# Layer 1's weighted sums on column tiles of 64 and 32 instead of 65 columns in one piece

## The chip, the cores and the metric

The kernel runs on one core of a Trainium2 chip. The metric is device time in microseconds (us), smaller is better. A core has five engines that run their own instruction streams side by side: TensorE (PE, matrix products into the accumulation memory PSUM; its weight loads are listed apart as PEld), VectorE (DVE), ScalarE (ACT), GpSimd (POOL) and SyncE (SP, which only issues transfers here). Semaphores tie the streams together.

## The reference

A stack of four graph layers over 4096 nodes with 64 features and one 4096 x 4096 adjacency of zeros and ones. Every layer normalises x, applies a ReLU, computes something from the neighbours and adds it to x. The change concerns layer 1, which works on every pair of nodes in hyperbolic space:

```
x_t     = logmap0(x, c)
left    = x_t @ w_att[:D, 0];  right = x_t @ w_att[D:, 0]
adj_att = sigmoid(left[:, None] + right[None, :] + b_att[0]) * adj
x_local = logmap(x[:, None, :], x[None, :, :], c)
support_t = einsum('ij,ijd->id', adj_att, x_local)
return proj(expmap(x, support_t, c), c)
```

The 64-vector `logmap(x_i, x_j)` is a scalar that depends on the pair times a combination of x_i and x_j. So the einsum becomes, for every node i, a sum over j of (weight of the pair) times a row of 65 numbers of node j: its 64 features and one more from its squared norm. The distance part of the weight is the same for (i, j) and (j, i); the sigmoid and the adjacency are not. Layers 0, 2 and 3 are not touched.

## The kernel before

Layer 0 takes the first 1240 us, layer 1's pairs 1240 to 1832 us, a chain of VectorE work on the nodes (`finish`) up to about 1904 us, layers 2 and 3 the rest. All times here are counted in the profiled execution.

The pairs are computed in `pairs_fast`. The nodes form 8 groups of 512 (`G`), each four blocks of 128 (`GB` = 4). A job is a pair of groups (gi, gj) with gj <= gi, 36 jobs in all: 28 off the diagonal and 8 on it. Each job computes the symmetric factor once, in four steps that the code writes as functions over batches of two jobs:

- `scores` / `weights_of`: mask and attention logits go to PSUM by two matmuls per block (`pl`, lines 2194 and 2197), and ScalarE takes the sigmoid into `sg`, for both directions of the pair.
- `distances`: four f32 matmuls (`pu`, line 2225), clipped by VectorE (line 2232) and combined (line 2233).
- `factors`: four wide passes on ScalarE and two on VectorE (lines 2247 and 2252) give the factor `F_`.
- `sums`: VectorE multiplies the weights by the factor (line 2260). Four f32 matmuls with the 65-column rows of the source nodes as weights (`XQ`, the same tile as `VQ`) add into `acci` (line 2262). Off the diagonal the factor is transposed block by block on TensorE (`pf`, line 2277), multiplied into the weights of the other direction (line 2280), and four more matmuls add into `accj` (line 2281); VectorE then adds `accj` to `VT` (line 2288). When the diagonal job closes group gi, `acci` is copied to `VT` (line 2270).

`VT` holds the 65 sums in partitions 0 to 64 and the nodes along the free dimension. After the pairs it is brought back to nodes-in-partitions form by 32 transposes (line 2312), and VectorE scales the result into `VQ` (line 2314).

The PSUM pools hold two buffers each for `pu`, `pl` and `pf`, and one each for `acci` and `accj`.

The order of the instructions on TensorE and VectorE is not the order of these lines. The framework's scheduler places each engine's instructions by its own costs; only ScalarE's activations (`act`) are held in program order. TensorE's stream around the sums is therefore an interleaving of `pl`, `pu`, `pf`, `acci` and `accj` work.

An f32 matmul is two instructions in the profile ("pieces" below), each with its own weight load, which is why the 144 matmuls of line 2262 appear as 288.

Of the kernel before, what the change touches and what calls it, by code (L numbers as in the profile page):

```python
# [9 lines left out]
F32 = mybir.dt.float32  # L10
# [8 lines left out]
ALU = mybir.AluOpType  # L19
# [5 lines left out]
P = 128  # L25
N = 4096
NB = N // P
D = 64
G = 512
NG = N // G  # L30
GB = G // P
# [799 lines left out]
def kernel(  # L831
# [24 lines left out]
    nc = tc.nc  # L856
# [7 lines left out]
    D1 = D + 1  # L864
# [10 lines left out]
    ident = cpool.tile([P, P], F32, name="ident")  # L875
# [45 lines left out]
    def over(col, width):  # L921

        return col.unsqueeze(2).to_broadcast([P, col.shape[1], width])
# [75 lines left out]
    with ExitStack() as l0:  # L999
# [281 lines left out]
        with ExitStack() as pa:  # L1281
            hp = pa.enter_context(tc.tile_pool(name="prep", bufs=1))
            work = pa.enter_context(tc.tile_pool(name="pwork", bufs=2))
# [47 lines left out]
            with in_order():  # L1331
                nc.vector.tensor_reduce(fsum, FT[0:F, :], AX.X, ALU.add)
                for b0 in range(0, NB, 8):
                    pw = (ps, ps2)[b0 // 8 % 2].tile([P, 8, KZ], F32, name="pst", tag="misc")
                    for b in range(8):
                        nc.tensor.matmul(
                            pw[:, b, :],
                            lhsT=FT[:, (b0 + b) * P : (b0 + b + 1) * P],
                            rhs=rhz,
                            start=True,  # L1340
                            stop=True,
# [19 lines left out]
                for g in range(HW // G):  # L1361
                    pr = (ps, ps2)[g % 2].tile([P, G], F32, name="psr", tag="misc")
                    nc.tensor.matmul(
                        pr, lhsT=srep, rhs=FT[:, g * G : (g + 1) * G], start=True, stop=True
# [27 lines left out]
                for k in range(2):  # L1392
                    pr = ps.tile([P, G], F32, name="prs", tag="misc")
                    for q in range(4):
# [3 lines left out]
                            lhsT=rs,  # L1398
                            rhs=FT[:, g * G : (g + 1) * G],
                            start=True,  # L1400
                            stop=True,
# [23 lines left out]
        with ExitStack() as ha:  # L1425
            hp = ha.enter_context(tc.tile_pool(name="heads", bufs=2))
            work = ha.enter_context(tc.tile_pool(name="hwork", bufs=1))
# [32 lines left out]
            for hf in range(2):  # L1460
# [9 lines left out]
                for hd in range(NH):  # L1470
                    first = hd == 0
# [47 lines left out]
                    def add_up(acc, values, moving, start, stop):  # L1519
                        for k in range(NS):  # L1520
                            ins = nc.tensor.matmul(  # L1521
                                acc[k * O : (k + 1) * O, :],
                                lhsT=values,
                                rhs=moving(k),
                                start=start,
                                stop=stop,
                            )
                        return ins.ins
# [3 lines left out]
                    for j0 in range(0, NB, 2):  # L1532
# [19 lines left out]
                        for i, j in enumerate(range(j0, j0 + 2)):  # L1552
                            for n, (acc, y) in enumerate(parts):
# [4 lines left out]
                                    start=j == 0 and (n == 0 or acc is not parts[n - 1][0]),  # L1558
                                    stop=j == NB - 1 and (acc is not accB or n == len(parts) - 2 - spatial),
                                )  # L1560
                        for i, j in enumerate(range(j0, j0 + 2)):
                            for c in range(2):
# [5 lines left out]
                                    start=j == 0 and c == 0,  # L1568
                                    stop=False,
                                )  # L1570
                                if whole:
# [4 lines left out]
                                        start=False,  # L1576
                                        stop=False,
                                    )
                            if first:
                                with behind(sums):  # L1580
# [6 lines left out]
                                        start=(j == 0),  # L1587
                                        stop=(j == NB - 1),
# [15 lines left out]
                    if first:  # L1604
# [3 lines left out]
                        pf = ps.tile([P, GB, NS, NH], F32, name="pf", tag="misc")  # L1608
                        for b in range(GB):
                            nc.tensor.matmul(  # L1610
                                pf[:, b].rearrange("p q h -> p (q h)"),
                                lhsT=dsum[:, b * P : (b + 1) * P],
                                rhs=fold_f.rearrange("p q h -> p (q h)"),
                                start=True,
                                stop=True,
# [11 lines left out]
                    for c in range(2):  # L1627
                        for k in range(NS):
                            nc.tensor.matmul(
                                accC[k * O : (k + 1) * O, :],  # L1630
                                lhsT=meanq[k * O : (k + 1) * O, hd, c, :],
                                rhs=em4[k * O : (k + 1) * O, :],
                                start=False,
                                stop=c == 1,
# [92 lines left out]
        with ExitStack() as ob:  # L1727
            hp = ob.enter_context(tc.tile_pool(name="outatt", bufs=1))
            work = ob.enter_context(tc.tile_pool(name="owork", bufs=2))
# [44 lines left out]
            with in_order():  # L1774
# [67 lines left out]
                for k in reversed(range(NK)):  # L1842
                    r = (NK + k) * O
# [68 lines left out]
            for u in range(4):  # L1912
# [8 lines left out]
                for q in range(NQ):  # L1921
# [10 lines left out]
                    for t in range(0, JT, 2):  # L1932
# [12 lines left out]
                        for acc, Y, E in products:  # L1945
                            for i in range(2):
                                for k in range(NK):
                                    sums = nc.tensor.matmul(
                                        acc[k],
                                        lhsT=Y[:, i].rearrange("p s d -> p (s d)"),  # L1950
                                        rhs=E[:, i, k * G : (k + 1) * G],
                                        start=j0 + i == 0,
                                        stop=acc is accB and j0 + i == NB - 1,
                                    )
                    with behind(sums.ins):
                        for t in range(JT):
                            j = q * JT + t
                            fl = dict(start=(j == 0), stop=(j == NB - 1))
                            for k in range(NK):
# [3 lines left out]
                                    lhsT=YD1[:, j],  # L1963
                                    rhs=B2[t // 2][:, t % 2, ks],
# [4 lines left out]
                                    lhsT=YD2[:, j],  # L1969
                                    rhs=m[:, t, ks].bitcast(F8),  # L1970
# [14 lines left out]
                for k in range(NK):  # L1985
                    nc.tensor.matmul(
                        accC[k],
                        lhsT=meano[NK * O :, k].rearrange("p s d -> p (s d)"),
                        rhs=em[NK * O :],
                        start=False,  # L1990
                        stop=True,
# [114 lines left out]
    def pairs_fast(es, VQ):  # L2106

        fp = es.enter_context(tc.tile_pool(name="pf", bufs=1))
        XQ = VQ
# [11 lines left out]
        with ExitStack() as ss:  # L2121
# [16 lines left out]
            pt = ps.tile([3 * NB, P], F32, name="ppt", tag="misc")  # L2138
# [10 lines left out]
            for dst, k in ((XA, 0), (LD, 1)):  # L2149
# [11 lines left out]
                for g in range(NG):  # L2161
# [4 lines left out]
                        ps,  # L2166
                        nc.scalar.copy,
                    )
        VT = fp.tile([D1, N], F32, name="VT")
        work = es.enter_context(tc.tile_pool(name="pfwork", bufs=2))  # L2170
        with ExitStack() as ss:
            ps_u = ss.enter_context(tc.tile_pool(name="ps_u", bufs=2, space=PSUM))
            ps_l = ss.enter_context(tc.tile_pool(name="ps_l", bufs=2, space=PSUM))
            ps_f = ss.enter_context(tc.tile_pool(name="ps_f", bufs=2, space=PSUM))
            ps_a = ss.enter_context(tc.tile_pool(name="ps_a", bufs=1, space=PSUM))

            def grp(g):
                return slice(g * G, (g + 1) * G)
# [30 lines left out]
            accs, sig, tiles = {}, {}, {}  # L2209
# [26 lines left out]
            def factors(batch):  # L2236
# [12 lines left out]
                for job in batch:  # L2249
                    at, xt = tiles[job]  # L2250
                    act(at, at, AF.Ln, bias=one_t, scale=1.0)
                    nc.vector.scalar_tensor_tensor(at, at, TMAX, xt, ALU.min, ALU.mult)

            def sums(batch):
                for gi, gj in batch:
                    F_ = tiles.pop((gi, gj))[0]
                    if gj == 0:
                        accs[gi] = ps_a.tile([D1, G], F32, name="acci", tag="acci")
                    w = sig.pop((gi, gj))
                    nc.vector.tensor_tensor(w, w, F_, ALU.mult)  # L2260
                    for b in range(GB):
                        nc.tensor.matmul(  # L2262
                            accs[gi],
                            lhsT=XQ[:, gj * GB + b, :],
                            rhs=w[:, b, :],
                            start=(gj == 0 and b == 0),
                            stop=(gi == gj and b == GB - 1),
                        )
                    if gi == gj:
                        nc.vector.tensor_copy(VT[:, grp(gi)], accs.pop(gi))  # L2270
                        continue
                    w = sig.pop((gj, gi))
                    accj = ps_a.tile([D1, G], F32, name="accj", tag="accj")
                    for t in range(GB):
                        pf = ps_f.tile([P, G], F32, name="pf", tag="pf")
                        for b in range(GB):
                            nc.tensor.transpose(
                                pf[:, b * P : (b + 1) * P], F_[:, b, t * P : (t + 1) * P], ident
                            )
                        nc.vector.tensor_tensor(w[:, t, :], w[:, t, :], pf, ALU.mult)  # L2280
                        nc.tensor.matmul(
                            accj,
                            lhsT=XQ[:, gi * GB + t, :],
                            rhs=w[:, t, :],
                            start=(t == 0),
                            stop=(t == GB - 1),
                        )
                    nc.vector.tensor_tensor(VT[:, grp(gj)], VT[:, grp(gj)], accj, ALU.add)


# [13 lines left out]
                    distances(batches[n + 2])  # L2304

        nc.vector.tensor_scalar(pabs, pabs, sqc, 2.0, ALU.mult, ALU.mult)
        with tc.tile_pool(name="ps_vt", bufs=2, space=PSUM) as ps:
            for g in range(NG):
                pt = ps.tile([P, GB, D1], F32, name="pvt", tag="misc")
                for b in range(GB):  # L2310
                    c = (g * GB + b) * P
                    nc.tensor.transpose(pt[:, b, :], VT[:, c : c + P], ident[:D1, :D1])
                bs = slice(g * GB, (g + 1) * GB)
                nc.vector.tensor_tensor(VQ[:, bs, :], pt, over(pabs[:, bs], D1), ALU.mult)

# [333 lines left out]
    with tc.If(general == 0):  # L2649
        after_pairs(pairs_fast)  # L2650
        with ExitStack() as es:
            layers_fast(es)
        nc.vector.tensor_reduce(bad[:, 0:1], bad, AX.X, ALU.add)
        odd = spool.tile([P, 1], F32, name="odd")
        nc.gpsimd.partition_all_reduce(odd, bad[:, 0:1], P, RMAX)
        nc.vector.tensor_scalar(again, odd, 0.0, None, ALU.is_gt)
# [57 lines left out]
```

## Time and profile before

| | us |
|---|---|
| median of 3 runs (2250.61 to 2261.21) | 2261.08 |
| the profiled execution's own time | 2264.45 |
| its span | 2262.7 |
| stretch of the pairs, 1240 to 1832 us | 592 |
| of this: TensorE busy | 549.1 |
| VectorE busy | 504.9 |
| ScalarE busy | 488.4 |

The span is the time from the first to the last instruction on the profiled core. "Busy" of TensorE is the union of its matmul records; their ends are modelled, so what is trustworthy is the distance from the start of one record to the start of the next. A row of a group gives line, engine, operation, output and inputs, shapes as partitions x elements, the count, busy time and mean duration, then the idle time of the engine just before these instructions and what ended it. "128*65" in a row of TensorE is contraction by columns used of the array.

### The profile page before, as it was taken

The page shows a single profiled execution, that of the slowest core. Times are in us where ns is not written, and L with a number is a line of the kernel's source. Part 1 is how long each engine was busy: PE and PEld are TensorE (multiplying, and loading weights), DVE is VectorE, ACT ScalarE, POOL GpSimd, SP SyncE. Part 2 cuts the span into 40 slices and gives each one's busy share as a digit, 9 for nine tenths or more (in the row PEclk, how much of TensorE's full clock was granted, in tenths as well). Part 3 has the DMA queues.
Part 4 walks back from the last instruction along what each step waited for, and adds up shares of the span by engine and source line. Part 5 has one row for each costly group of instructions (what it writes and reads, how often), then busy time and mean ns, then how long its engine had stood idle before and what let it go on. Part 6 is the DMA issues. An engine that isn't in the chain of part 4 may idle for free. (4 is left out here: it accounts for less than half of the span.)

```text
span 2262.7 us, 42590 instructions
## 1 busy us (share of the span) xinstructions
PE 1938.4 (86%) x18732; PEld 904.9 (40%) x18732; DVE 1770.1 (78%) x2074; ACT 1589.8 (70%) x1338; POOL 86.0 (4%) x124
## 2 busy tenths in 40 slices
PE   4989989999999999859992799999999933959998
PEld 3444444444444544423441244434344411434332
DVE  6689989987898899797657888888898889544552
ACT  4678878996898899467752888879788920114775
POOL 1000100100000000001101000000000000000000
PEclk8999999999999999879995899999999966965999
DMA  9945554352111020477530001100110005724993
GB/s 112 181 89 104 90 90 114 123 190 93 44 63 63 26 75 2 132 247 264 188 122 20 20 23 33 38 24 28 33 33 26 26 0 204 301 82 140 332 332 119
DMA packets 117002, 238.92 MB, mean 106 GB/s; under 512 B 11059, under 2 KB 84003, under 8 KB 102051
## 3 DMA queue, kind: packets, MB, share of 16 engines
q1 hardware_dynamic: 101990, 192.92, 24.6%
q0 software_dynamic: 14816, 43.18, 10.8%
q8 instruction: 148, 2.42, 0.4%
q14 instruction: 48, 0.39, 0.1%
HBM read 245.34 MB, written 49.46 MB: 130 GB/s over the span
## 5 line engine op out<-in xcount | busy, mean ns | idle before, releaser
L1185 ACT ACTIVATE st<-srow,nt 128x2048 int8<-128x2048 f32 x352 | 682.8, 1994 | 81.6 <-DVE B L1191 80.8
L1191 DVE TENSOR_TENSOR B<-st,mres 128x1024 int32<-128x1024 int32 x256 | 312.0, 1221 | 71.8 <-PE accC L1521 44.6
L1521 PE MATMUL accB<-B,ybh 128*32 128x512 fp8e4 x3072 | 340.5, 385 | 15.6 <-DVE B L1191 15.6
L1521 PE MATMUL accD<-B,ybh 128*32 128x512 fp8e4 x2048 | 302.6, 388 | 23.6 <-DVE h L1637 23.6
L1521 PEld LDWEIGHTS <-ybh 128*32 128x32 bf16 (+1 forms) x6656 | 197.5, 98 | 240.8 <-issue 79.8
L1521 PE MATMUL accC<-B,ycn 128*32 128x512 fp8e4 x2272 | 267.8, 380 | 1.2 <-issue 1.2
L1521 PE MATMUL accC<-mres,ych 128*32 128x512 fp8e4 x2272 | 268.0, 381 | 0.0
L1521 PE MATMUL accL<-B,ybh 128*32 128x512 fp8e4 x1536 | 221.4, 391 | 4.8 <-DVE h L1641 4.7
L1521 PEld LDWEIGHTS <-ych 128*32 128x32 f16 x4096 | 169.0, 99 | 116.5 <-issue 11.9
L929 DVE SCALAR_TENSOR_TENSOR raw<-raw 128x2048 f32<-128x2048 f32 x64 | 146.4, 2289 | 79.3 <-DMA raw<-in_adj_dram 79.1
L1179 DVE TENSOR_SCALAR st<-srow,nt 128x2048 uint8<-128x2048 f32 x160 | 205.6, 1285 | 2.5
L2181 ACT ACTIVATE sg<-pl,rb 128x512 f32<-128x512 f32 x256 | 163.6, 684 | 53.7 <-PE pl L2197 50.6
L1185 ACT ACTIVATE st<-srowo,nto 128x1024 int8<-128x1024 f32 x128 | 137.3, 1137 | 42.1 <-DVE B L1191 42.1
L2225 PE MATMUL pu<-XAf,LDf 66*128 66x512 f32 x288 | 151.4, 630 | 13.7 <-DVE at L2232 12.5
L2607 ACT ACTIVATE w3b<-pv 128x1024 int16<-128x1024 f32 x128 | 131.1, 1024 | 45.6 <-PE pv L2598 45.3
L1521 PE MATMUL accC<-C,ych 128*32 128x512 fp8e4 x1824 | 148.3, 393 | 1.4 <-DVE C L1199 1.4
L1199 DVE TENSOR_TENSOR C<-B,mres 128x1024 int32<-128x1024 int32 x114 | 139.6, 1225 | 3.6
L2262 PE MATMUL acci<-sg,VQ 128*65 128x512 f32 x288 | 137.8, 602 | 4.8 <-DVE sg L2260 4.6
L1521 PEld LDWEIGHTS <-ycn 128*32 128x32 f16 x2272 | 107.6, 97 | 64.0 <-issue 3.1
L2416 PE MATMUL nacc<-m,HH 128*128 128x512 fp8e4 x256 | 62.0, 391 | 74.6 <-ACT HH L2405 74.6
L2232 DVE TENSOR_SCALAR at<-pu 128x512 f32<-128x512 f32 x144 | 95.2, 685 | 26.2 <-PE pu L2225 26.2
L2194 PE MATMUL pl<-nm,noid 128*128 128x512 fp8e4 x256 | 101.0, 395 | 11.8 <-ACT sg L2181 11.7
(488 smaller groups left out, 3124.3 us busy)
## 6 DMA issues: line engine op xcount, KB each, us to landing
raw<-in_adj_dram SPq DMA_DIRECT2D x64, 1024.0 KB, 6.9
mo<-edges SPq DMA_DIRECT2D x32, 512.0 KB, 4.7
noedge<-nmo POOLq DMA_DIRECT2D x32, 512.0 KB, 4.3
nm<-noedge SPq DMA_DIRECT2D x64, 256.0 KB, 3.1
m<-edges SPq DMA_DIRECT2D x16, 1024.0 KB, 5.2
m<-edges SPq DMA_DIRECT2D x32, 512.0 KB, 5.0
srow<-srow_d SPq DMA_DIRECT2D x15, 1024.0 KB, 6.6
mres<-in_adj_dram POOLq DMA_DIRECT2D x8, 1024.0 KB, 35.7
```

Source lines behind the costliest of these rows:

```text
L929: nc.vector.scalar_tensor_tensor(raw, raw, 0.0, raw, ALU.is_gt, ALU.not_equal, accum_out=bad[:, c : c + 1])
L1179: nc.vector.tensor_scalar(st[:, i, :].bitcast(U8), srow, negs[:, i : i + 1], EDGE, ALU.is_gt, ALU.mult)
L1185: nc.scalar.activation(st[:, i, :], srow, AF.Sign, bias=negs[:, i : i + 1], scale=-1.0)
L1191: nc.vector.tensor_tensor(B.bitcast(I32), st.bitcast(I32), edges.bitcast(I32), ALU.bitwise_and)
L1199: nc.vector.tensor_tensor(C.bitcast(I32), B.bitcast(I32), edges.bitcast(I32), ALU.bitwise_xor)
L1521: ins = nc.tensor.matmul(acc[k * O : (k + 1) * O, :], lhsT=values, rhs=moving(k), start=start, stop=stop,)
L2181: tc.keep_in_program_order(nc.scalar.activation(*args, **kw))
L2194: nc.tensor.matmul(pl, lhsT=noid, rhs=nm[:, b, :].bitcast(F8), start=True, stop=False)
L2225: nc.tensor.matmul(pu, lhsT=LD[:, j * P : (j + 1) * P], rhs=XA[:, grp(gi)], start=True, stop=True,)
L2232: nc.vector.tensor_scalar(at[:, b, :], pu, UMIN, None, ALU.max)
L2262: nc.tensor.matmul(accs[gi], lhsT=XQ[:, gj * GB + b, :], rhs=w[:, b, :], start=(gj == 0 and b == 0), stop=(gi == gj and b == GB - 1),)
L2607: nc.scalar.activation(w, pv, AF.Relu)
```

## The change

`VT` becomes a tile of 128 partitions. A helper `add_up` issues one matmul either with the 64 feature columns of a source block (`row` is None: 64 output rows at partition `low`, a column tile of 64) or with columns 33 to 64 of its row (32 output rows at partition `row`, a column tile of 32), of which only the last, the 65th, is of use.

Off the diagonal, `accj` has the features of one direction in partitions 0 to 63 and the 32-wide tiles in partitions 64 and 96; `acci` has the features of the other in partitions 64 to 127 and the 32-wide tiles in partitions 0 and 32. For every block t the two 64-wide matmuls stand behind each other in the code, and after every second block the four 32-wide ones. On the diagonal both accumulators are used too: even blocks go to `accj`, odd ones to `acci`. When a diagonal job closes a group, two copies of 64 partitions bring `acci` to `VT` with its halves exchanged, and `accj` is added as in the other jobs.

The 32 transposes of `VT` become 32 f32 matmuls with a 128 x 65 matrix `fold_v` that adds the two halves and picks the two rows of the 65th column; two small VectorE instructions build it.

```diff
-        VT = fp.tile([D1, N], F32, name="VT")
+        VT = fp.tile([P, N], F32, name="VT")
...
+            def add_up(acc, low, row, src, w, start, stop):
+                cols, r, n = (slice(0, D), low, D) if row is None else (slice(D1 - 32, D1), row, 32)
+                nc.tensor.matmul(
+                    acc[r : r + n, :], lhsT=XQ[:, src, cols], rhs=w, start=start, stop=stop
+                )
...
-                    for b in range(GB):
-                        nc.tensor.matmul(
-                            accs[gi],
-                            lhsT=XQ[:, gj * GB + b, :],
-                            rhs=w[:, b, :],
...
                     if gi == gj:
-                        nc.vector.tensor_copy(VT[:, grp(gi)], accs.pop(gi))
-                        continue
+                        for b in range(0, GB, 2):
+                            j = gj * GB + b
+                            add_up(accj, 0, None, j, w[:, b], b == 0, b == GB - 2)
+                            add_up(acci, D, None, j + 1, w[:, b + 1], gi == 0 and b == 0, b == GB - 2)
                         for b in range(GB):
+                            j = gj * GB + b
+                            r = b // 2 * 32
+                            if b % 2:
+                                add_up(acci, 0, r, j, w[:, b], gi == 0, True)
+                            else:
+                                add_up(accj, 0, D + r, j, w[:, b], True, True)
+                        accs.pop(gi)
+                        nc.vector.tensor_copy(VT[0:D, grp(gi)], acci[D : 2 * D])
+                        nc.vector.tensor_copy(VT[D : 2 * D, grp(gi)], acci[0:D])
+                    else:
+                        v = sig.pop((gj, gi))
+                        for t in range(GB):
...
+                            nc.vector.tensor_tensor(v[:, t, :], v[:, t, :], pf, ALU.mult)
+                            first = gj == 0 and t == 0
+                            add_up(accj, 0, None, gi * GB + t, v[:, t], t == 0, t == GB - 1)
+                            add_up(acci, D, None, gj * GB + t, w[:, t], first, False)
+                            if t % 2:
+                                for k in range(2):
+                                    c = t - 1 + k
+                                    last = c + 2 >= GB
+                                    add_up(accj, 0, D + k * 32, gi * GB + c, v[:, c], t == 1, last)
+                                    add_up(
+                                        acci, 0, k * 32, gj * GB + c, w[:, c], gj == 0 and t == 1, False
+                                    )
                     nc.vector.tensor_tensor(VT[:, grp(gj)], VT[:, grp(gj)], accj, ALU.add)
...
+        fold_v = work.tile([P, D1], F32, name="fold_v", bufs=1)
+        nc.vector.tensor_copy(fold_v[:, 0:D], ident[:, 0:D])
+        nc.vector.tensor_tensor(
+            fold_v[:, D:], ident[:, D + 31 : D + 32], ident[:, P - 1 :], ALU.add
+        )
...
-                    nc.tensor.transpose(pt[:, b, :], VT[:, c : c + P], ident[:D1, :D1])
+                    nc.tensor.matmul(
+                        pt[:, b, :], lhsT=VT[:, c : c + P], rhs=fold_v, start=True, stop=True
+                    )
```

More of the change, by code (lines that the diff above doesn't have):

```diff
@@ L2257, in sums @@
                     if gj == 0:
-                        accs[gi] = ps_a.tile([D1, G], F32, name="acci", tag="acci")
+                        accs[gi] = ps_a.tile([P, G], F32, name="acci", tag="acci")
+                    acci = accs[gi]
+                    accj = ps_a.tile([P, G], F32, name="accj", tag="accj")
                     w = sig.pop((gi, gj))
                     nc.vector.tensor_tensor(w, w, F_, ALU.mult)
-                    for b in range(GB):
-                        nc.tensor.matmul(
-                            accs[gi],
-                            lhsT=XQ[:, gj * GB + b, :],
-                            rhs=w[:, b, :],
-                            start=(gj == 0 and b == 0),
-                            stop=(gi == gj and b == GB - 1),
-                        )
@@ L2269, in sums @@
-                    if gi == gj:
-                        nc.vector.tensor_copy(VT[:, grp(gi)], accs.pop(gi))
-                        continue
[L2272 to L2275, printed above, removed]
-                        for b in range(GB):
[L2277 to L2287, printed above, removed]
+                    if gi == gj:
+                        for b in range(0, GB, 2):
+                            j = gj * GB + b
+                            add_up(accj, 0, None, j, w[:, b], b == 0, b == GB - 2)
+                            add_up(acci, D, None, j + 1, w[:, b + 1], gi == 0 and b == 0, b == GB - 2)
+                        for b in range(GB):
+                            j = gj * GB + b
[10 more added lines that the diff above has]
+                        for t in range(GB):
+                            pf = ps_f.tile([P, G], F32, name="pf", tag="pf")
+                            for b in range(GB):
+                                nc.tensor.transpose(
+                                    pf[:, b * P : (b + 1) * P], F_[:, b, t * P : (t + 1) * P], ident
+                                )
[11 more added lines that the diff above has]
+                                    )
@@ L2311, in pairs_fast @@
                     c = (g * GB + b) * P
-                    nc.tensor.transpose(pt[:, b, :], VT[:, c : c + P], ident[:D1, :D1])
+                    nc.tensor.matmul(
+                        pt[:, b, :], lhsT=VT[:, c : c + P], rhs=fold_v, start=True, stop=True
+                    )
                 bs = slice(g * GB, (g + 1) * GB)
```

## The prediction

> **What bounds the kernel now.** I first cut the span into stretches and asked each engine's busy time there. Columns: stretch and its length, then busy time (instructions) of PE, PEld, DVE, ACT, POOL, granted clock, DMA share, GB/s. The first row is the whole stretch of the pairs, the second runs from the first to the last sum.
>
> ```profile
> 1240.00:1832.00 592.00, 549.07 (x1792) 234.07 (x1792) 504.91 (x444) 488.44 (x438) 0.00 (x0) 0.95 0.10 29
> 1281.30:1828.60 547.30, 520.37 (x1699) 221.66 (x1700) 471.33 (x412) 456.71 (x411) 0.00 (x0) 0.95 0.10 28
> ```
>
> TensorE is busy 520.4 of 547.3 us (95%), VectorE 471.3 (86%), ScalarE 456.7 (83%); DMA is a tenth busy. TensorE is the bound, with VectorE 49 us behind it. After the stretch `finish` is a VectorE chain that needs all of VQ, so the end of the last sum moves the end of the kernel one for one.
>
> Next the groups by line, for the sums' share of TensorE, and the waits in the stretch (engine and line, what ended the wait: us in total, times, longest).
>
> ```profile
> L2225 PE MATMUL pu<-XAf,LDf 66*128 66x512 f32 x288 | 151.4, 630 | 13.7 <-DVE at L2232 12.5 <-ACT LDf L962 1.2
> L2262 PE MATMUL acci<-sg,VQ 128*65 128x512 f32 x288 | 137.8, 602 | 4.8 <-DVE sg L2260 4.6
> L2281 PE MATMUL accj<-sg,VQ 128*65 128x512 f32 x224 | 109.0, 603 | 0.4 <-DVE sg L2280 0.4
> ...
> ACT sg L2181 <- PE pl L2197: 48.6, 90, 1.8
> DVE sg L2280 <- PE pf L2277: 24.3, 20, 2.2
> PE pl L2194 <- ACT sg L2181: 10.8, 27, 1.8
> ```
>
> ScalarE and VectorE wait for TensorE far longer than it waits for them. The sums hold 137.8 + 109.0 = 246.8 us of it. The timeline (start, us, engine, line, count) gives the real price of a piece:
>
> ```profile
> 1562.76 3.60 PE L2262 MATMUL acci<-sg,VQ 128*65 128x512 f32 x8
> 1566.19 1.88 PE L2281 MATMUL accj<-sg,VQ 128*65 128x512 f32 x4
> ```
>
> Eight pieces from 1562.76 to 1566.19 are 0.429 us each, so a matmul is 0.858 us at full clock. I call this a unit. The 256 matmuls of before are 256 units, 219.6 us; the rows' 246.8 us hold the lower clock and modelled ends too.
>
> **What the Trainium skill says.** "TensorEngine Tiling (Array Packing)", Theoretical Speedup, gives up to 2x for 64 columns and 4x for 32. The trace agrees for fp8 on four 32-column tiles: sets of four start at 400.43 and 400.64 us.
>
> ```profile
> 400.43 0.40 PE L1521 MATMUL accD<-B,ybh 128*32 128x512 fp8e4 x4
> 400.64 0.40 PE L1521 MATMUL accB<-B,ybh 128*32 128x512 fp8e4 x4
> ```
>
> No f32 matmul of before runs on column tiles. The same page, Key Properties: "Changing tiling mode (not just tile) drains the TensorE". In layer 2 full-width and 32-column matmuls alternate:
>
> ```profile
> 1913.18 3.63 PE L2416 MATMUL nacc<-m,HH 128*128 128x512 fp8e4 x16
> 1916.74 1.05 PE L2428 MATMUL dc<-m,sel 128*32 128x512 fp8e4 x16
> 1917.72 0.60 PE L2416 MATMUL nacc<-m,HH 128*128 128x512 fp8e4 x2
> ```
>
> A round takes 1917.72 - 1913.18 = 4.54 us; sixteen full ones and four sets of four at 0.2155 us are 4.31, so a switch costs (4.54 - 4.31)/2 = 0.115 us. "TensorE: Matmul & The Clock Gate", Part 3 (The mechanism), says matmuls are strict FIFO in start and end; no record above contradicts this. So two tiles overlap only if they are neighbours in TensorE's stream.
>
> **The change part by part.** As written, the 256 matmuls become 256 of 64 columns in 128 pairs (128 units) and 256 of 32 columns in 64 fours (64 units): 192 units, 55 us less. But the scheduler orders the stream, and in the changed program's instruction order the partners are mostly apart. A common run ("i" is acci, "j" accj, then tile width @ first column):
>
> ```
> i32@32  i64@64 i64@64  i32@0  j64@0 j64@0  j32@64 j32@96   then pf transposes
> ```
>
> Neighbours on the same columns queue behind each other. Only 12 of the 64-wide matmuls, and 96 of the 32-wide, stand directly behind one of equal width on other columns. The 512 matmuls form 123 runs between full-width work (246 switches) with 190 changes between 64 and 32 inside the runs: 436 switches; before had none in this stretch.
>
> I price the groups of equal width. A group on one tile costs one unit per matmul. In a chain on alternating tiles, the second piece of one overlaps the first piece of the next: a chain of n costs (n + 1)/2 units. 64-wide: 52 + 39 groups of two on one tile (182), 41 + 15 single (56), 3 pairs (4.5), 3 chains of four (7.5): 250 units. 32-wide: 42 + 36 single (78), 54 + 18 pairs (108), 6 of three (12), 4 of four (10): 208. Together 458 units, 393.0 us.
>
> - Sums: 393.0 - 219.6 = +173.4 us.
> - Switches: 436 x 0.115 = +50.1 us. f32 weight loads on tiles may not hide there (0.138 us each before); none of that to all of it is +0 to +60, and I take 0, because loads at the fp8 switch show none.
> - Fold: before, eight transposes per 0.66 us (timeline, 1828.43), so 0.08 each; 32 f32 matmuls are 64 pieces, about 32 x 0.1 = 3 us more, half issued ahead of the last sums: +2 us.
> - VectorE: 8 more copies and 8 more adds at 0.68 us (rows of lines 2270 and 2288), 11 us on 471, hidden as TensorE stays ahead. Without that cover they would cost up to 11. The two for fold_v issue at the stretch's start, below 1 us.
> - New waits: the diagonal now starts accj, so its first matmul waits for the VectorE add of the previous accj (one buffer); queued behind it on TensorE are pf and pl, for which VectorE and ScalarE wait. At 0.7 us an add, 8 x 0.7 = 6 us at most. I take 0: other sums stand between in the order.
> - Given back: TensorE idles 26.9 us of the 547 and loses 5% of clock, 27 us. With TensorE further ahead of the others, part goes: bounds 0 and 54, I take 25.
>
> Transfers, ScalarE's work and all stages outside are unchanged.
>
> Sum: 173.4 + 50.1 + 2 - 25 = +201 us. Against the profiled execution's 2264.45 that is 2465; its time is 3.4 above the median, so 2462.
>
> **The rivals.**
> - *Width changes are free* (only 128 to tiled drains, 64 and 32 overlap on different columns). Walking the runs in FIFO order that way gives 381.5 units, 327.3 us: +107.7 + 246 x 0.115 (28.3) + 2 - 25 = +113, 2374. For it: the tiles are still separate columns. Against: the page's "mode".
> - *f32 doesn't overlap on column tiles at all*: 512 units, 439.3 us: +219.7 + 50.1 + 2 - 25 = +247, 2508; without give-back 2533. For it: no f32 case before, and f32 moves four times the bytes of fp8 per column. Against: two f32 tiles of 4 bytes would read in 0.429 us just what four fp8 tiles read in two sets, 0.431 us.
> - *Each column tile has its own queue*: the same runs, with only the columns deciding, give 255 units (218.8 us): no gain, +28.3 for switches, +2, and 0 to 25 given back: +5 to +30, 2280.
> - *Faster: partners meet across the stream.* Place: the runs of line 2260. If the array let a matmul overtake waiting ones and short full-width work and switches cost nothing, 192 units would be near: -55; VectorE's 471 + 11 us allow it. Some 10 us of new VectorE waits leave -45, 2216. It decides once the sums with their switches take under 256 units; with 436 switches (59 units) that is under 197, against 458 counted. The strict FIFO speaks against it.
>
> **How the numbers follow.** Drained and FIFO (2462): 45%. No f32 overlap (2508): 22%. Width changes free (2374): 20%. Own queues (2280): 8%. Faster (2216): 5%. The likeliest alone spans 2433 to 2487 (give-back 54 and 0). For 8 in 10 the range takes in no-overlap up to 2535, and free width changes with give-back nearly full, 2350; own queues and faster are left out. A measurement can tell about 0.5% (11 us) from no change: own queues falls a quarter inside that, faster a fifth; so faster 4%, same 3%, slower 93%.
>
> **What would show it.** Right: the pairs' stretch near 790 us with TensorE at 95% or more, VectorE near 65%; the row of `acci` and `accj` at line 2260 with 1024 pieces; two pieces on the same columns 0.43 us apart, pieces on different columns of equal width starting together; about 0.1 us lost at each change of width; later stages as long as before, only shifted. Wrong: different-width neighbours starting together (free changes); partners in sequence throughout (no overlap); a `j64@0` starting before the second `i64@64` ahead of it has (own queues); or TensorE below 90% busy because VectorE's products come late in the new order.

## The result and the profile after

The changed kernel takes 2454.14 us (median of 4 runs, 2452.59 to 2457.18) against 2260.11 for the kernel before: ratio 1.087, interval 1.0839 to 1.0902. The prediction was 2462, with 2350 to 2535 as its range.

The stretches of the profile after, cut at the first and the last sum (columns as in the prediction: stretch, busy time and instructions of PE, PEld, DVE, ACT, POOL, granted clock, DMA share, GB/s), and then what follows to the end:

```profile
1275.70:2011.80 736.10, 705.33 (x2249) 224.21 (x2249) 486.24 (x432) 457.98 (x411) 0.00 (x0) 0.97 0.07 21
2011.80:2450.70 438.90, 324.42 (x1638) 137.77 (x1636) 238.48 (x299) 168.69 (x211) 16.47 (x26) 0.79 0.55 195
```

The stretch of the sums grew from 547.3 to 736.1 us, and nearly all of it is TensorE: it is busy for 705.3 us (96%) where it had 520.4. VectorE has 15 us more work than before and is down to 66%. The rest of the kernel takes 438.9 us; before it was 434.1. So the loss is where the prediction put it.

The groups by line (busy, mean ns, then idle before):

```profile
L2260 PE MATMUL acci<-sg,VQ 128*64 128x512 f32 (+1 forms) x512 | 232.5, 611 | 1.3 <-DVE VT L2289 1.3
L2260 PE MATMUL accj<-sg,VQ 128*64 128x512 f32 (+1 forms) x512 | 192.9, 612 | 6.2 <-DVE sg L2274 4.6 <-DVE VT L2310 1.6
L2227 PE MATMUL pu<-XAf,LDf 66*128 66x512 f32 x282 | 148.4, 634 | 11.3 <-DVE at L2234 11.3
```

And the waits of the stretch (engine and line, what ended the wait: us in total, times, longest):

```profile
ACT sg L2183 <- PE pl L2199: 125.0, 96, 4.7
DVE sg L2298 <- PE pf L2295: 106.0, 43, 8.8
DVE VT L2310 <- PE accj L2260: 86.5, 25, 8.7
```

The two groups of sums, 1024 pieces as forecast, are busy 425 us if the rows are added; before they were 247. Were each `accj` piece beside an `acci` piece, the two rows would cover the same microseconds; at 232.5 and 192.9 us in a total of 396 us (below) they overlap for only some 30 us. The other two engines wait for TensorE far longer than before (125 us where ScalarE waited 48.6, 106 where VectorE waited 24.3). The distances (the `pu` row, of which 282 of 288 pieces fall into this window) take 634 ns a piece where they took 630.

What the sums cost is read from starts: the time from the start of each sum's piece to the start of TensorE's next matmul, summed over the trace.

| kernel | sums, us | transposes, pl and pu, us | TensorE idle, us | first to last sum, us |
|---|---|---|---|---|
| before | 224.6 | 321.1 | 26.9 | 546.8 |
| after | 395.8 | 333.4 | 30.7 | 735.5 |

Here and below, "sums" in a table or a result is this time. Idle time is contained in the other columns. The sums took 171 us more, the full-width work 12 more, and the matmuls of the fold that now lie inside the stretch 5. Together that is the 189 us.

Grouped by neighbours of equal width, the sums of the after trace look like this ("i" acci, "j" accj, then column; the time runs to the start of what follows, and so includes the change of width behind the group):

```
width 64  i64 i64 or j0 j0     91 groups   1.861 us
width 64  one alone            56 groups   1.003 us
width 64  j0 and i64            3 groups   1.010 us
width 32  one alone            78 groups   0.976 us
width 32  two on two columns   72 groups   0.983 us
width 32  four on four          4 groups   0.996 us
```

(The columns come from the program's order, the times from the trace. Nine rarer groups, of three 32-wide or four 64-wide, are left out.) Two on one tile take twice 0.858 and a change; two on different tiles take hardly more than one. The timeline shows tiles that overlap, and one that has no partner. First the 32-wide tiles: the last of three first pieces, and then the second pieces of the same three matmuls (start, us, engine, line, count):

```profile
1613.03 0.62 PE L2260 MATMUL acci<-sg,VQ 128*32 128x512 f32 x1
1613.47 0.60 PE L2260 MATMUL accj<-sg,VQ 128*32 128x512 f32 x2
1613.48 0.59 PE L2260 MATMUL acci<-sg,VQ 128*32 128x512 f32 x1
1614.01 0.66 PE L2295 MATMUL pf<-ident,at 128*128 128x128 f32 x4
```

The pieces at 1613.47 and 1613.48 belong to three matmuls on three tiles; they run together, and the transposes can start 0.54 us later. Then a single 64-wide matmul between full-width ones:

```profile
1602.72 0.38 PE L2199 MATMUL pl<-MOV,one 128*128 128x512 bf16 x1
1603.03 1.07 PE L2260 MATMUL accj<-sg,VQ 128*64 128x512 f32 x2
1604.04 0.39 PE L2196 MATMUL pl<-nm,noid 128*128 128x512 fp8e4 x1
```

From 1602.72 to 1604.04 are 1.32 us. The `pl` takes 0.215 of them, as the `pl` ahead of it did, and the two pieces 0.858, so the two changes cost 0.247 us, 0.12 each. This matmul had no partner. It took as long as the 65-column one of before, and the changes came on top.

### The profile page after: what moved, and what is told of

Read it like the earlier page. It is cut to its first block, busy times and chain, and to the rows that moved or that the text cites. A ratio compares the mean times of both kernels' runs of the same rounds, so it can differ in the third digit from the quotient of the medians.

```text
span 2450.7 us, 43729 instructions
## 1 busy us (share of the span) xinstructions
PE 2123.4 (87%) x19276; PEld 906.8 (37%) x19276; DVE 1783.7 (73%) x2092; ACT 1590.7 (65%) x1338; POOL 86.0 (4%) x124
## 4 chain that ended last, share of the span: by engine, by line
PE 43%; DVE 13%; DMA 6%; issue 4%; ACT 2%; POOL 0%; DVEq 0%; SPq 0%; POOLq 0%; ACTq 0%
PE acci L2260 8%; PE accj L2260 7%; DMA raw<-in_adj_dram 4%; PE pu L2227 4%; PE acco L1948 4%; PE pl L2196 2%; PE pf L2295 2%; PE nacc L2445 2%; PE pl L2199 2%; DVE raw L929 2%; PE accC L1521 1%; DVE at L2254 1%; PE tr L961 1%; PE accB L1521 1%; PE ddo L1961 1%
## 5 line engine op out<-in xcount | busy, mean ns | idle before, releaser
L2260 PE MATMUL acci<-sg,VQ 128*64 128x512 f32 (+1 forms) x512 | 232.5, 611 | 1.3 <-DVE VT L2289 1.3
L2260 PE MATMUL accj<-sg,VQ 128*64 128x512 f32 (+1 forms) x512 | 192.9, 612 | 6.2 <-DVE sg L2274 4.6
L2298 DVE TENSOR_TENSOR sg<-sg,pf 128x512 f32<-128x512 f32 x112 | 74.6, 684 | 106.1 <-PE pf L2295 106.0
L2183 ACT ACTIVATE root<-xt,consts 128x2048 f32<-128x2048 f32 x36 | 71.8, 1994 | 100.2 <-DVE at L2249 100.2
```

Source lines behind the costliest of these rows:

```text
L2183: tc.keep_in_program_order(nc.scalar.activation(*args, **kw))
L2260: nc.tensor.matmul(acc[r : r + n, :], lhsT=XQ[:, src, cols], rhs=w, start=start, stop=stop)
L2298: nc.vector.tensor_tensor(v[:, t, :], v[:, t, :], pf, ALU.mult)
```

## The experiments

The theory ("A" in the expectations) is that the tiles do overlap, but the scheduler's order puts partners apart and changes width 436 times. The first four kernels test it. In all tables "units" are counted in the program's order under the rule that the trace of after shows, full overlap of neighbours of equal width on different columns; a unit is 0.858 us.

**Tie the sums in issue order.** The same matmuls, each issued behind the one before it in the code:

```diff
-                nc.tensor.matmul(
+                ins = nc.tensor.matmul(
                     acc[r : r + n, :], lhsT=XQ[:, src, cols], rhs=w, start=start, stop=stop
-                )
+                ).ins
+                if chain:
+                    tc.add_manual_dep(
+                        ins,
+                        chain[-1].name,
...
+                        reason="sums_in_order",
+                    )
+                chain[:] = [ins]
```

> The changed kernel, with one edit: every matmul of the sums is tied in issue order to the one before it in the code, so partners on other columns are neighbours in TensorE's stream. Same matmuls, same 1024 pieces. The stream then has 197 units (0.858 us each) and 245 changes of width or to full width, against 407 and 437 for the changed kernel when partners overlap fully, as its trace shows (before: 256 and 0). Theory A (the order separates the partners): the sums take 197 x 0.858 + 245 x 0.115 = 197 us instead of 400 (before: 220). 2238 if nothing else binds, up to 2265 if VectorE's latency shows; taken: 2250. Rival B (narrow f32 matmuls and their double number of pieces cost by themselves, in whatever order): stays at 2420 or more.

Measured: 2253.91 us, ratio to before 0.9997 (0.9978 to 1.0016). All of the 194 us came back with not one matmul changed. The sums take 204.6 us by starts (forecast 197), and their two rows have the same length and cover the same microseconds:

```profile
L2260 PE MATMUL accj<-sg,VQ 128*64 128x512 f32 (+1 forms) x512 | 203.8, 633 | 17.0 <-DVE sg L2310 6.9 <-DVE VT L2322 5.4 <-DVE sg L2286 4.6
L2260 PE MATMUL acci<-sg,VQ 128*64 128x512 f32 (+1 forms) x512 | 203.2, 633 | 0.0
```

Rival B is out: narrow f32 matmuls and their double count of pieces are not what cost the 194 us. But the kernel is no faster than before. Its sums are 20 us shorter than before's, its stretch from first to last sum only 9 us (537.9 for 546.8), and that is less than its own executions differ (2237.33 to 2261.26 us).

**Leave out the 32-wide matmuls.** The sum of the 65th column is left out; the order is the scheduler's.

```diff
+        nc.gpsimd.memset(VT[D:, :], 0.0)
...
-                            if t % 2:
-                                for k in range(2):
...
-                        for b in range(GB):
-                            j = gj * GB + b
-                            r = b // 2 * 32
...
-                        nc.vector.tensor_copy(VT[D : 2 * D, grp(gi)], acci[0:D])
-                    nc.vector.tensor_tensor(VT[:, grp(gj)], VT[:, grp(gj)], accj, ALU.add)
+                    nc.vector.tensor_tensor(VT[0:D, grp(gj)], VT[0:D, grp(gj)], accj[0:D], ALU.add)
```

> The changed kernel without the 32-column matmuls: the sum of the 65th column is left out (its place holds zeros), so 256 of the 512 matmuls go; the order is again the scheduler's own. The stream has 240 units and 191 changes. Theory A: the 64-column half alone, in the scheduler's order, costs 240 x 0.858 + 191 x 0.115 = 228 us, that is 172 less than the changed kernel and 8 more than before: 2275 to 2295, taken 2283. So the 65th column would carry nearly all of the loss, and the 64-column tiles would gain nothing for lack of neighbours. Rival C (tiles of 64 overlap as written and only the 65th column is dear): 128 units, some 90 us less, bounded by VectorE, 2200 to 2215.

Measured: 2328.91, ratio 1.0348 (1.0301 to 1.0395). Rival C is out: half of the matmuls are gone and it is still slower than before, with sums of 234.3 us (forecast 228) where pairs would take 110. The forecast of the total missed by 46 us, and not in the sums: the full-width work took 369.7 us by starts instead of the 333.4 of after, with idle time of 53.8 instead of 30.7, at a granted clock of 0.92 in the stretch instead of 0.97. The 65th column was expected to carry nearly all of the loss. Leaving it out gave back 161 of the 171 us that the sums had lost, but only 125 of the kernel's 194, because TensorE waited more and its clock was lower. The last section shows how the two go together.

**Gather each job's sums.** As the tied kernel, but all four transposes of a job first, then its eight 64-wide matmuls, then its eight 32-wide ones.

```diff
                             nc.vector.tensor_tensor(v[:, t, :], v[:, t, :], pf, ALU.mult)
+                        for t in range(GB):
                             first = gj == 0 and t == 0
                             add_up(accj, 0, None, gi * GB + t, v[:, t], t == 0, t == GB - 1)
                             add_up(acci, D, None, gj * GB + t, w[:, t], first, False)
-                            if t % 2:
...
+                        for c in range(GB):
+                            k = c % 2
+                            last = c + 2 >= GB
+                            add_up(accj, 0, D + k * 32, gi * GB + c, v[:, c], c < 2, last)
+                            add_up(acci, 0, k * 32, gj * GB + c, w[:, c], gj == 0 and c < 2, False)
```

> As the chained kernel, but off the diagonal all four transposes and products of a job come first, then its eight 64-column matmuls, then its eight 32-column ones: 206 units, 206 changes, 200 us for the sums. Theory A: within 10 us of the chained kernel; 2238 to 2270, taken 2252. If changes of width cost much more than 0.115 us each (rival D), it gains 39 of them back against the chained one and is faster by over 5 us. Rival B: 2420 or more.

Measured: 2248.78, ratio 0.998 (0.9963 to 0.9997), sums 202.8 us. It is 5 us from the tied kernel, at the edge of what rival D named; the intervals of the two overlap. The next kernel separates better.

**No change between 64 and 32.** The tied kernel with the 65th column on tiles of 64 too (columns 1 to 64 of the row).

```diff
-                cols, r, n = (slice(0, D), low, D) if row is None else (slice(D1 - 32, D1), row, 32)
+                cols, r, n = (slice(0, D), low, D) if row is None else (slice(D1 - D, D1), row, D)
...
-                                    add_up(accj, 0, D + k * 32, gi * GB + c, v[:, c], t == 1, last)
+                                    add_up(accj, 0, D, gi * GB + c, v[:, c], c == 0, c == GB - 1)
```

> As the chained kernel, but the 65th column is summed on tiles of 64 columns too (columns 1 to 64 of the row, of which the last is of use), so nothing changes between 64 and 32: 266 units and 171 changes to and from full width. Theory A: 266 x 0.858 + 171 x 0.115 = 248 us for the sums, 28 more than before: 2280 to 2300, taken 2289, and about 45 more than the chained kernel, the price of a fourth unit for each three. Rival B (narrow pieces cost by themselves): 2400 or more. Rival D (changes of width are what costs): below the chained kernel.

Measured: 2282.47, ratio 1.0146 (1.0108 to 1.0184), sums 245.9 (forecast 248). It has 74 changes fewer than the tied kernel and 69 units more, and is slower; rival D is out. Units and changes at 0.115 us account for the sums of after and of all four kernels:

| kernel | units | changes | sums forecast, us | sums by starts, us | first to last sum, us | whole, us |
|---|---|---|---|---|---|---|
| after | 407 | 436 | 399 | 395.8 | 735.5 | 2454.14 |
| tied | 197 | 245 | 197 | 204.6 | 537.9 | 2253.91 |
| without the 65th column | 240 | 191 | 228 | 234.3 | 613.4 | 2328.91 |
| by job | 206 | 206 | 200 | 202.8 | 530.9 | 2248.78 |
| all on 64 | 266 | 171 | 248 | 245.9 | 567.5 | 2282.47 |

(The forecast of after is made with the trace's rule, the others' before they ran. Part of a change falls into the full-width work around the sums.)

**A control, and what is left to gain.** Four more kernels ask whether the tie helps by itself, whether a better order beats both kernels, and what binds then. The first ties the 65-column sums of the kernel before and changes nothing else:

```diff
-                        nc.tensor.matmul(
+                        held(nc.tensor.matmul(
                             accs[gi],
...
-                        )
+                        ))
```

> The kernel before, with nothing but the same tie in issue order on its 256 sums of 65 columns. A control for the tie itself. Theory A: no tiles, so 256 units and no changes, and within 0.5% of before (2243 to 2265). Rival G (the chained kernels owe their recovery to the order on TensorE as such, not to tiles that overlap): faster than before by 0.5% or more, and then the tiles add nothing.

Measured: 2254.62, ratio 0.9997 (0.9978 to 1.0015). The tie by itself does nothing, so rival G is out: what the tied kernel wins against after, it wins by overlap (197 units where there were 407) and, for some 22 us, by fewer changes of width (245 where there were 436).

The second holds the first sum of a job behind the job's last transpose, so that its eight 64-wide matmuls stand together:

```diff
-                                nc.tensor.transpose(
+                                pfs = nc.tensor.transpose(
...
+                        chain.append(pfs)
                         for t in range(GB):
                             first = gj == 0 and t == 0
```

> The by-job kernel with one more tie: the first 64-column matmul of a job is issued behind the job's last transpose, so the eight stand together. 193 units and 154 changes, 183 us for the sums (before: 220; chained: 197; by job: 200). Theory A: 14 to 17 us less TensorE work than the chained and by-job kernels; as the chained one kept 9 of its 20 us in the pairs' stretch, because VectorE (482 us) comes close, 2225 to 2245 against a kernel before of 2254, taken 2237, ratio 0.9925. Rival F (VectorE is already the bound): same as by job within 3 us.

Measured: 2236.43, ratio 0.991 (0.9883 to 0.9937). This is faster than both kernels, with the sums at 188.4 us. Rival F is out. The new tie is an entry of the same chain, so the first sum of a job waits for two instructions. The stretch of the sums, in the columns of the first view:

```profile
1278.60:1799.00 520.40, 487.44 (x2249) 192.21 (x2249) 480.03 (x430) 456.38 (x411) 0.00 (x0) 0.98 0.10 29
```

And its groups of sums:

```profile
L2260 PE MATMUL acci<-sg,VQ 128*64 128x512 f32 (+1 forms) x512 | 190.6, 617 | 0.0
L2260 PE MATMUL accj<-sg,VQ 128*64 128x512 f32 (+1 forms) x512 | 190.6, 617 | 9.5 <-DVE sg L2286 4.6 <-DVE VT L2321 4.6 <-DVE sg L2310 0.2
```

Again the two rows are equal, 190.6 us each, and they are the same microseconds: TensorE is busy 487.4 us in all. VectorE is at 480.0 of 520.4, 92%. The profiled execution is the fastest of seven (2225.53 us, 11 below their median). So its 27 us against before's stretch are not to be read as the gain, which by the medians is 20 us.

The third is the tied kernel without the 65th column (left out as above), to see how far less TensorE work could bring it:

```diff
+                if chain:
+                    tc.add_manual_dep(
+                        ins,
+                        chain[-1].name,
...
-                            if t % 2:
-                                for k in range(2):
...
```

> The chained kernel without the 32-column matmuls (the sum of the 65th column is left out): 129 units and 131 changes, 126 us for the sums, 94 less than before and 108 less than measured without the tie (234). TensorE then has some 410 us of work in the stretch. Theory A: VectorE (476 us) becomes the bound, and the stretch ends at about 505, 40 us less than before: 2200 to 2225, taken 2213. Rival H (TensorE's work alone sets the end): about 2254 - 94 = 2160.

Measured: 2241.99, ratio 0.9927 (0.9897 to 0.9958). Its sums take 131.1 us, 57 less than the contiguous kernel's, and it is not faster. Rival H is out, and the theory's 2213 was 29 too low. Its stretch of the sums:

```profile
1280.60:1803.70 523.10, 465.13 (x1737) 189.34 (x1737) 476.04 (x423) 457.11 (x411) 0.00 (x0) 0.90 0.10 29
```

The longest of TensorE's waits for VectorE in it (of its weight loads, us in total, times, longest):

```profile
PEld pu L2228 <- DVE at L2235: 43.8, 36, 2.6
PEld accj L2261 <- DVE sg L2303: 36.5, 60, 2.3
```

VectorE is at 91%, TensorE waits for it, and TensorE's granted clock is 0.90 where the contiguous kernel had 0.98; `pu` takes 167.9 us by starts against 132.1 there. The work taken from TensorE came back as idle time (57.9 us against 32.9) and as a lower clock. Whether one of these two holds the floor near 520 us, or the order of VectorE's work, I didn't separate.

The fourth takes 11 us from VectorE by moving the copies of `acci` to ScalarE:

```diff
-                        nc.vector.tensor_copy(VT[0:D, grp(gi)], acci[D : 2 * D])
-                        nc.vector.tensor_copy(VT[D : 2 * D, grp(gi)], acci[0:D])
+                        tc.keep_in_program_order(nc.scalar.copy(VT[0:D, grp(gi)], acci[D : 2 * D]))
+                        tc.keep_in_program_order(nc.scalar.copy(VT[D : 2 * D, grp(gi)], acci[0:D]))
```

> The contiguous kernel with the 16 copies of acci into VT moved from VectorE to ScalarE, held in ScalarE's program order (195 units, 144 changes, 184 us). VectorE loses 11 us of 482. If VectorE bounds the contiguous kernel, 4 to 11 us less than it; if TensorE still does, the same within 3 us. Taken: 4 less, 2233.

Measured: 2267.87, ratio 1.0045 (1.0026 to 1.0063), so 31 us slower than the contiguous kernel and a miss. Its sums are as short (188.7 us), but TensorE idles 40.3 us instead of 32.9 and has a clock of 0.93 in the stretch instead of 0.98, and `pu` takes 156.0 us by starts. The copies stand in ScalarE's order behind the factor's passes, and `acci` has one buffer. In one of the groups the last sum, the first copy and the next sum into `acci` start so:

```profile
1600.28 0.59 PE L2260 MATMUL acci<-sg,VQ 128*32 128x512 f32 x1
1616.47 0.58 ACT L2300 COPY VT<-acci 64x512 f32<-64x512 f32 x1
1621.05 1.12 PE L2260 MATMUL acci<-sg,VQ 128*64 128x512 f32 x1
```

The first copy starts 16.2 us after the last piece of the sum. In the first seven groups such distances add up to 71 us where the contiguous kernel, with VectorE's copies, has 9. In four of these groups the next sum follows 2.6 to 3.5 us behind the end of the second copy, and of the 7.4 us more that TensorE idles, 7.1 lie between the last sum of a group and the next one. So the late copies do hold up the sums. The lower clock costs more than this idle time; that it comes from the late copies too is argued.

## Why the prediction was right, step by step

- *TensorE is the bound and the end moves one for one.* Right. The profiled span grew by 188.0 us; the stretch from first to last sum by 188.7.
- *The order puts partners apart.* Right, and the cause: tying the same matmuls in order took back all 194 us.
- *Sums, 458 units.* Too many. The rule for a chain of n on alternating tiles, (n + 1)/2 units, was wrong: the first pieces of all partners run together and then the second pieces, so a pair takes one unit (0.983 us with its change for two 32-wide ones) and not one and a half. By the trace's rule the same stream has 407 units, 349 us in place of 393. This term was 44 us too large.
- *Switches, 436 x 0.115 = 50.1.* Right. The trace shows 0.145 us behind a 64-wide group, 0.118 behind a 32-wide one and about 0.095 on entering from full width, which add up to some 53 us. "TensorEngine Tiling (Array Packing)", Key Properties, says that a change of mode drains the engine; here it does so between 64 and 32 columns as well, and the trace gives the price. The bound of +60 for weight loads that don't hide was not needed.
- *Given back, 25.* Wrong: on balance nothing was. TensorE idled 30.7 us instead of 26.9, and the clock's loss, counted as in the prediction, went from 27 us (5% of 547) to 22 (3% of 736). This error hid more than half of the 44 us that the chain rule had added too much, and so the total came within 8 us of the measurement. That the order decides and the price of a switch were right; how several tiles share a unit and what is given back were wrong in opposite directions, so the closeness of the total is partly luck.
- *Fold, +2; VectorE, 0; new waits, 0.* Small, as forecast. 48 of the fold's 64 pieces lie inside the stretch and take 5 us more there than the transposes did; from the last sum to layer 2's first matmul are 77.2 us where there were 78.1. Together that is some 4 us. Two things that the change doesn't touch cancel: the first sum comes 5.5 us earlier, and layers 2 and 3 took 6 us longer in this execution.
- *The rivals.* Widths that change for free: out, the 0.145 us are lost behind a 64-wide group also when a 32-wide one follows. No overlap of f32: out by the groups' times. A queue for each tile, and partners that meet across the stream: out, two matmuls on one tile take two units (1.861 us with the change, in 91 groups) though partners stand a little further on in the stream. The gain that the faster rival stood for does exist, but only if the stream is ordered for it, and then 0.9% of the kernel.

## What to carry to other kernels

Column tiling paid here only for neighbours in TensorE's stream. So look at the order that the scheduler made, count groups of equal width, units and changes of width, and multiply by two measured times. Here this gave the sums of five kernels within 8 us each, while the totals were off by up to 46 us where waits and clock moved too. If the scheduler separates partners, tie them in issue order and gather them into long runs. Then look at the next engine: here the gain stopped at a stretch of some 520 us, with VectorE busy for 91 to 92% of it.

## What the runs showed that I had not expected

- f32 matmuls on different column tiles overlap fully, although each is two pieces on the same tile: the first pieces of two to four partners start within 0.02 us of each other, and so do the second, 0.45 to 0.48 us later at full clock. Four 32-wide ones take 0.996 us with the change of width, one takes 0.976. Whether the pieces stood interleaved in the stream or overtook each other can't be told from the trace.
- TensorE's clock was lower where TensorE waited more, and the waits come first. Seven kernels idle 26 to 33 us in the stretch and have a granted clock of 0.95 to 0.98 there. The three with 40.3 us (copies on ScalarE), 53.8 and 57.9 us (without the 65th column) have 0.93, 0.92 and 0.90, and full-width matmuls that nobody had touched took longer in them. It is not the amount of work: the contiguous kernel and the one with copies on ScalarE have the same matmuls. In this stretch of all ten traces the clock falls to 0.50 for 3.4 us or a multiple of that, up to four times, and 84 of these 86 drops begin within 5.1 us of the start of a TensorE wait longer than 1 us. Not every such wait, of 121, is followed by one. No experiment lengthened waits alone, so this is an order in time, not a proof.
